# Head squares on GpSimd, an earlier centring, a later scaling and a shorter last norm in a two-block transformer kernel

## The chip, the cores and the metric

The kernel runs on one core of a Trainium2 chip. A core has five engines that work side by side, each with its own queue of instructions: TensorE (PE in the profile, PEld for its weight loads), VectorE (DVE), ScalarE (ACT), GpSimd (POOL) and SyncE (SP), which here issues the DMA transfers. They wait for each other by semaphores. The metric is the time of one launch in microseconds (us), as the median of several runs.

## The reference, cut to what matters

Everything is float32. A batch of B = 8 elements, each 512 tokens by 256 features, goes through two transformer blocks. The change touches block 0 alone, whose core is this (16 heads of 16 features each):

```python
h = modulate(ln(x), shift_sa, scale_sa)
q = ln(_heads(h, H)) * qn_w + qn_b          # a norm per token and head
k = ln(_heads(h, H)) * kn_w + kn_b
v = _heads(h, H)
attn = softmax(einsum('bhqd,bhkd->bhqk', q, k) * scale)
x = x + gate_sa[:, None, :] * unheads(einsum('bhqk,bhkd->bhqd', attn, v))
# cross-attention: q from modulate(ln(x), shift_ca, scale_ca), k and v from 64 context tokens
x = x + gate_ca[:, None, :] * (cross_attention(x) @ ca_out_w.T + ca_out_b)
h = modulate(ln(x), shift_ff, scale_ff)
x = x + gate_ff[:, None, :] * (silu(h @ w1.T) * (h @ w3.T) @ w2.T)
```

Each `ln` takes away the mean and divides by the standard deviation. `ln(_heads(h))` does so for each of the 16 features of a head, for 512 x 16 pairs of token and head. Block 1 has the same three stages with wider heads, and follows.

## The kernel before, in words

**Slots.** Block 0 is laid out by hand over slots. A cycle has 18 slots (`CYCLE`), one cycle for each batch element and two more to finish. In cycle b, `batch1(b)` does the self-attention of element b. Its 16 attention blocks (four groups g of four heads' work each, four pieces kt of the keys) fill the slots 0 to 8, 10 to 12 and 14 to 17. Slots 9 and 13 (`X0`, `X1`) hold the two cross-attention blocks of element b-1, which `batch2(b-1)` arranges. `batch3(b-2)` does the feed-forward part of element b-2 in the same cycle (for elements 5 and 6 three slots later, for element 7 two slots earlier). So three elements are in work at a time: in cycles 2 to 6 there are self-attention, cross-attention, feed-forward and the preparation of the next element. Cycles 0 and 1 have no feed-forward; from cycle 8 on there is no self-attention.

**Order.** `at(i, fn)` puts a piece of work beside slot i. A slot first issues the scores of its own block (TensorE) with their exponentials (ScalarE), then the values of the block before it, and then the pieces beside it in the order in which they were registered: all of `batch1`, then `batch2`, then `batch3`. The order of the instructions on TensorE, VectorE, ScalarE and GpSimd is exactly this written order; only the order of the DMA issues on SP is left to a planner. An instruction whose input is not ready holds up whatever is written behind it for the same engine.

**The head norm.** For elements from 1 on it is prepared in the cycle before. In slots counted from that cycle's start: `norm(0)`, `norm(1)`, `norm(2)` in 7, 8 and 9 (statistics of x, the layer norm into `ln`, then modulation on GpSimd into `h`, L504 and L506); `head_rows` in 12 (GpSimd zeroes the padding columns of the tile `zx`, L521); `head_centre` for both halves of the heads in 12 (VectorE: sums L528, means L529, and L530, which writes h minus mean into `zx`); `head_var` in 13 (ScalarE squares `zx` into `ln`, L536; VectorE sums, L538, and scales, L539); `head_scale` in 14 (GpSimd: a power, L545, and a product into `zx`, L546). Two slots before each group starts, `queries_keys(g)` transposes a part of `zx` on TensorE (L554) and makes q (ScalarE, L557) and k (VectorE, L558). For group 0 of the next element that is slot 16 of the cycle before; for groups 1, 2 and 3 it is slots 2, 6 and 12 of its own cycle. The tiles `zx` and `ln` have a single buffer each.

**PSUM.** `bank_x()` deals out PSUM banks in turn: two of the tag X and then one of the tag D. The transposes, projections and feed-forward steps all take theirs from it.

**Feed-forward.** `up(f)`, beside slot 8+f, multiplies by two weights on TensorE into two banks, takes tanh on ScalarE (L773), and then VectorE forms the products (L774 and L775), which read the banks and so free them. `down(t)` in slots 16 to 19 multiplies back, and `add_gated` (L460, L462) adds to x.

**Cross-attention.** `batch2(b)`, whose slots count from cycle b+1: `prepare(0..2)` in slots 3, 4, 5 (norm of x into z: statistics L199 and L201, the power L175, the normalisation L208; then on GpSimd the gate row, L675, and its addition to x, L437), `turn` in 6 (transposes of z, L416, and modulation, L417), `queries(0)` and `queries(1)` in 7 and 8, the blocks at `X0` and `X1`, `inverse(c)` three slots after its block (reciprocal L721 of the softmax sums, and two DMAs that spread them, L724 and L726), and `scaled(c)` five slots after it (VectorE, L729). The projection out (L741) comes in slots 1 and 2 of the next cycle.

```python
at(i - 6, head_rows)
for c in range(2):
    at(i - 6, lambda c=c: head_centre(c))
    at(i - 5, lambda c=c: head_var(c))
    at(i - 4, lambda c=c: head_scale(c))
```

Here i is the first slot of the element's own cycle, so i-6 is slot 12 of the cycle before.

Of the kernel before, what the change touches and what calls it, by code (L numbers as in the profile page):

```python
# [12 lines left out]
AF = mybir.ActivationFunctionType  # L13
ALU = mybir.AluOpType
# [3 lines left out]
B, N, D, H, T, CD, FF = 8, 512, 256, 16, 64, 192, 1024  # L18
# [60 lines left out]
def fast_path(ctx: ExitStack, tc: tile.TileContext, a: dict, out: bass.AP):  # L79

    nc = tc.nc
# [393 lines left out]
    def at(i, fn):  # L475
        beside.setdefault(max(i, -1), []).append(fn)
# [5 lines left out]
    def batch1(b):  # L482
        s = {}
        base = CYCLE * b
# [38 lines left out]
        def head_centre(c, par=None):  # L523

            hv = s["hv"][:, :, 8 * c : 8 * c + 8] if par is None else s["hv"][:, :, 8 * c + par : 8 * c + 8 : 2]
            sh = [P, NT, hv.shape[2]]
            mean = small.tile(sh, F32, tag=f"mean{sh[2]}", name="mean", bufs=2)
            nc.vector.tensor_reduce(mean, hv, AX.X, ALU.add)  # L528
            nc.vector.tensor_scalar_mul(mean, mean, 1.0 / HD0)  # L529
            nc.vector.tensor_tensor(parts(s["z"][:, :, 0:D], c, par), hv,  # L530
                                    mean[:, :, :, None].to_broadcast([*sh, HD0]), ALU.subtract)

        def head_var(c, par=None):
            sq, z = parts(s["ln"], c, par), parts(s["z"][:, :, 0:D], c, par)
            sh = [P, NT, z.shape[2]]
            nc.scalar.activation(sq, z, AF.Square)  # L536
            s["var", c, par] = var = small.tile(sh, F32, tag=f"var{sh[2]}", name="var", bufs=2)
            nc.vector.tensor_reduce(var, sq, AX.X, ALU.add)  # L538
            nc.vector.tensor_scalar(var, var, 1.0 / HD0, EPS0, ALU.mult, ALU.add)  # L539
# [71 lines left out]
        n = 0  # L611
        for g in range(4):
            for kt in range(NT):
                while n in (X0, X1):
                    n += 1
                i = base + n
                blocks[i] = block(g, kt)
                if g == 0 and kt == 0:
                    if b == 0:
                        def before():  # L620
                            head_rows()
                            for n in range(3):
                                norm(n)
                            nc.vector.tensor_copy(qk_cols, cols[:, 0:2])
                            first_modulated(0, 0)
                            head_centre(0, 0)
                            head_var(0, 0)
                            head_scale(0, 0, nc.vector)

                        def gate():  # L630
                            spread(s["bc"][:, 2 * D : 3 * D], b, G_SA, D)

                        at(-1, before)
                        at(0, lambda: awake(3))
                        at(0, lambda: first_modulated(0, 1))
                        at(0, lambda: head_centre(0, 1))
                        at(1, lambda: head_var(0, 1))
                        at(1, lambda: head_scale(0, 1))
                        at(2, lambda: first_modulated(1))
                        at(3, lambda: head_centre(1))  # L640
                        at(4, lambda: head_var(1))
                        at(4, lambda: head_scale(1))
                        at(5, gate)
                    else:
                        for m in range(3):
                            at(i - 11 + m, lambda m=m: norm(m))
                        at(i - 6, head_rows)
                        for c in range(2):
                            at(i - 6, lambda c=c: head_centre(c))
                            at(i - 5, lambda c=c: head_var(c))  # L650
                            at(i - 4, lambda c=c: head_scale(c))
                if kt == 0:
                    at(i - 2, lambda g=g: queries_keys(g))
                if kt == NT - 1:
                    at(i + 1, lambda g=g: group_end(g))
                    at(i + 2, lambda g=g: group_back(g))
                n += 1


    def batch2(b):  # L660
        s = {}
        base = CYCLE * (b + 1)

        def prepare(n):

            if n == 0:
                s["gate"] = gate = wk2.tile([P, D], F32, tag="gate", name="gate", bufs=3)
                spread(gate, b, G_CA, D)
                s["pieces"] = normed_in_pieces(wk2, b, EPS0, lambda z: s.update(z=z))
            s["pieces"][n]()  # L670
            if n < 2:
                return
            gate = s["gate"]
            gb = wk2.tile([P, D], F32, tag="gb", name="gb", bufs=1)
            nc.gpsimd.tensor_tensor(gb, gate, row("cab0"), ALU.mult)  # L675
            add_row(b, gb)

        def turn():
            s["hT"] = transposed(wk2, s["z"], b, modT[:, 2:4, :], modT[:, 0:2, :])

        def queries(c):
            ps = bank_x()
            for k in range(2):
                mm(ps, w_q0[:, k, c * P : (c + 1) * P], s["hT"][:, k, :], k == 0, k == 1)
            s[c] = q = wk2.tile([P, N], F32, tag="q0", name="q0", bufs=2)
            nc.vector.tensor_scalar_add(q, ps, col("bq")[:, c : c + 1])

        def block(c):
            def score():
                pss = [bank_s() for _ in range(2)]  # L690
                for j in range(4):
                    r = slice(32 * j, 32 * j + 32)
                    mm(pss[j // 2][:, j % 2, :], kb0[r, c, b, :, :].rearrange("p e t -> p (e t)"), s[c][r, :])
                for u in range(2):
                    s["p", c, u] = p = wk.tile([P, 2, N], F32, tag="p", name="p", bufs=4)
                    nc.scalar.activation(p, pss[u], AF.Exp, scale=HD0 ** -0.5)

            def value():
                o = bank_x()
                for j in range(4):  # L700
                    mm(o[32 * j : 32 * j + 32, :], vb0[:, b, 4 * c + j, :, :].rearrange("p e d -> p (e d)"),
                       s["p", c, j // 2][:, j % 2, :])
                s["oT", c] = oT = wk2.tile([P, N], F32, tag="oT0", name="oT0")
                nc.scalar.copy(oT, o)

                d = bank_x()
                for j in range(4):
                    mm(d[32 * j : 32 * j + 32, :], sel0, s["p", c, j // 2][:, j % 2, :])
                den = wk2.tile([P, N], F32, tag="den", name="den", bufs=1)
                nc.scalar.copy(den, d)  # L710
                s["den", c] = dd = dram.tile([4, 2, N], F32, tag="den0", name="den0")
                for e in range(2):
                    nc.sync.dma_start(dd[:, e, :], den.rearrange("(j r) n -> j r n", j=4)[:, e, :])
                s["rec", c] = rec = wk2.tile([P, 8 * N // P], F32, tag="rec", name="rec", bufs=2)
                nc.sync.dma_start(rec, flat(dd))

            return Block([score], [value])

        def inverse(c):
            rec = s["rec", c]  # L720
            nc.vector.reciprocal(rec, rec)  # L721
            s["rb", c] = rb = wk2.tile([P, N], F32, tag="rb", name="rb", bufs=1)
            rd = dram.tile([4, 2, N], F32, tag="rec0", name="rec0")
            nc.sync.dma_start(flat(rd), rec)  # L724
            check(rec)
            nc.sync.dma_start(rb, rd.rearrange("j e n -> (j e) n")[:, None, :].to_broadcast([8, HD0, N]))  # L726

        def scaled(c):
            nc.vector.tensor_tensor(s["oT", c], s["oT", c], s["rb", c], ALU.mult)  # L729

        for n in range(3):
            at(base + 3 + n, lambda n=n: prepare(n))
        at(base + 6, turn)
        at(base + 7, lambda: queries(0))
        at(base + 8, lambda: queries(1))
        for c, n in enumerate((X0, X1)):
            blocks[base + n] = block(c)
            at(base + n + 3, lambda c=c: inverse(c))
            at(base + n + 5, lambda c=c: scaled(c))
        for qp in range(2):  # L740
            at(base + CYCLE + 1 + qp, lambda qp=qp: project_out(qp, lambda k: s["oT", k], w_o0, 2,  # L741
                                                            add_gated(wk2, b, s["gate"])))
# [1497 lines left out]
```

## Time and profile before

| what | value |
|---|---|
| three runs | 2454.86, 2447.49, 2453.35 us; median 2453.35 |
| the profiled execution | 2448.82 us |
| its span, first to last instruction | 2446.9 us, mean granted TensorE clock 0.997 |
| busy: TensorE, VectorE, ScalarE, GpSimd | 2408.0, 1058.9, 878.5, 858.5 us |
| block 0 (TensorE goes on to block 1 without a stop) | to about 864 us |
| TensorE idle, 180 to 740 us | 1.6 us of 560 |
| the head norm's squares, L536 | 17 on ScalarE |

The profile is one execution of the kernel, with the start and the length of every instruction. Its page gives the busy time by engine, the chain of work that ended last, and groups of equal instructions. Further views list what an engine waited for and who released it ("PE ps_S L109 <- DVE k L558" is a matmul of line 109 into `ps_S` that waited for VectorE's write of `k` by line 558), the busy times by stretches of the span together with the clock granted to TensorE (1.00 is full), and the instructions in order of time. Such a line gives start, length, engine, source line, operation, output and inputs, shape, the count of instructions merged into the line, and in brackets the idle time of the engine before it with its releaser. Line 109 is the helper through which all matmuls go; which work it is, the names of its tiles tell.

### The profile page before, as it was taken

What the parts mean: (1) busy time and instruction counts of PE and PEld (TensorE: products, weight loads), DVE (VectorE), ACT (ScalarE), POOL (GpSimd) and SP (SyncE); (2) the same over time, 40 slices, a digit from 0 to 9 for tenths busy, and PEclk for the clock granted to TensorE, in tenths of its full rate; (3) what the DMA queues carried; (4) which work ended last, traced back from release to release, by engine and by line L of the source; (5) the groups of instructions that cost most, each with busy time, mean ns of one, the idle gap of its engine ahead of it and who ended that gap; (6) DMA issues with size and microseconds to landing.
All of it is one profiled execution on the core that took longest, in us unless ns stands there. A gap on an engine that the chain in (4) does not pass through costs nothing.

```text
span 2446.9 us, 28449 instructions
## 1 busy us (share of the span) xinstructions
PE 2408.0 (98%) x10964; PEld 1157.3 (47%) x10964; DVE 1058.9 (43%) x2083; ACT 878.5 (36%) x1118; POOL 858.5 (35%) x538
## 2 busy tenths in 40 slices
PE   9999999999998999999999999999999999999999
PEld 4333443444435643444444444434345555566665
DVE  5544435434434434343434343434334766651210
ACT  4565545545452123333333333333332221222221
POOL 3443222222301026343434343434333444531110
PEclk9999999999999999999999999999999999999999
DMA  5120000000001000000000000000123222210000
GB/s 181 45 93 7 16 20 8 17 11 12 13 11 64 27 1 23 18 19 19 19 18 19 18 19 19 19 18 19 36 61 96 68 67 67 64 55 27 22 18 23
DMA packets 84400, 84.07 MB, mean 34 GB/s; under 512 B 42544, under 2 KB 58784, under 8 KB 84256
## 3 DMA queue, kind: packets, MB, share of 16 engines
q1 hardware_dynamic: 83352, 81.09, 10.6%
q8 instruction: 88, 1.44, 0.2%
q10 hardware_dynamic: 904, 1.07, 0.1%
q14 instruction: 56, 0.46, 0.1%
HBM read 72.09 MB, written 10.04 MB: 34 GB/s over the span
## 4 chain that ended last, share of the span: by engine, by line
PE 92%; DVE 3%; issue 1%; ACT 1%; DMA 1%; POOL 1%; SPq 0%; POOLq 0%; DVEq 0%; ACTq 0%
PE ps_X L109 38%; PE ps_S L109 23%; PE ps_O L109 14%; PE ps_D L109 14%; PE ps_X L416 1%; DVE t L836 1%; DMA rec<-rec 1%; DMA rb<-rec 1%; POOL p L1252 1%; ACT p L574 0%; PE ps_X L554 0%; PE ps_X L596 0%; PE ps_D L416 0%; DVE t L833 0%; ACT hT L417 0%
## 5 line engine op out<-in xcount | busy, mean ns | idle before, releaser
L109 PE MATMUL ps_S<-q,k 32*128 32x512 f32 (+1 forms) x3072 | 429.1, 625 | 7.3 <-ACT p L574 3.1
L1012 ACT ACTIVATE p<-ps_S 128x1024 f32<-128x1024 f32 x256 | 248.1, 1022 | 522.1 <-PE ps_S L109 522.1
L574 ACT ACTIVATE p<-ps_S 128x1024 f32<-128x1024 f32 x256 | 248.2, 1021 | 232.1 <-PE ps_S L109 230.7
L109 PEld LDWEIGHTS ps_S<-q,k 32*128 32x128 f32 (+1 forms) x3072 | 160.5, 184 | 233.1 <-issue 137.5
L991 DVE TENSOR_TENSOR t<-ps_X,rope_c 128x512 f32<-128x512 f32 x126 | 87.2, 692 | 349.9 <-PE ps_X L109 349.9
L1031 DVE TENSOR_TENSOR sm<-sm,p 128x1024 f32<-128x1024 f32 x128 | 190.6, 1532 | 59.2 <-ACT p L1012 59.2
L994 POOL TENSOR_TENSOR q<-t 128x512 f32<-128x512 f32 x32 | 40.8, 1276 | 406.6 <-DVE t L992 406.6
L175 POOL TENSOR_TENSOR rstd<-rstd,mhalf 128x4 f32<-128x4 f32 x49 | 51.0, 1042 | 326.8 <-DVE rstd L174 325.2
L1027 POOL TENSOR_TENSOR sm<-p 128x1024 f32<-128x1024 f32 x64 | 149.3, 2354 | 38.0 <-ACT p L1012 38.0
L109 PE MATMUL ps_X<-hT,w 128*128 128x512 f32 x344 | 160.5, 601 | 1.3 <-ACT hT L417 0.9
L837 POOL TENSOR_TENSOR q<-t,t 128x512 f32<-128x512 f32 x72 | 95.1, 1321 | 176.4 <-DVE t L836 172.4
L109 PE MATMUL ps_O<-p,h 128*32 128x512 f32 x1024 | 139.4, 614 | 1.6 <-ACT oT L587 1.6
L109 PE MATMUL ps_O<-p,v 128*64 128x512 f32 x512 | 138.0, 617 | 0.0
L109 PE MATMUL ps_D<-p,v 128*64 128x512 f32 x512 | 131.6, 592 | 0.0
L453 DVE TENSOR_TENSOR x<-ps_X,x 128x512 f32<-128x512 f32 x27 | 18.7, 692 | 239.4 <-PE ps_X L109 239.4
L109 PE MATMUL ps_X<-hT,w_sa_wq 128*128 128x512 f32 x256 | 115.9, 595 | 3.0 <-ACT hT L417 3.0
L109 PE MATMUL ps_X<-w_sa_wv,hT 128*128 128x512 f32 x256 | 118.0, 604 | 0.0
L109 PE MATMUL ps_X<-w_sa_wo,oT 128*128 128x256 f32 x512 | 114.5, 382 | 0.1
L545 POOL TENSOR_TENSOR var<-var,mhalf 128x32 f32<-128x32 f32 (+1 forms) x17 | 87.3, 5135 | 75.2 <-ACT t L773 41.7
L109 PE MATMUL ps_X<-hT,w_sa_wk 128*128 128x512 f32 x248 | 112.4, 596 | 0.0
L109 PE MATMUL ps_S<-hT,w_ff_w 128*128 128x512 f32 x256 | 111.3, 592 | 0.0
L109 PEld LDWEIGHTS ps_X<-w_sa_wo,oT 128*128 128x128 f32 x512 | 96.0, 190 | 24.2 <-issue 11.4
(282 smaller groups left out, 3537.0 us busy)
## 6 DMA issues: line engine op xcount, KB each, us to landing
rb<-rec SPq DMA_DIRECT2D x128, 128.0 KB
rb<-rec_d SPq DMA_DIRECT2D x124, 128.0 KB
rb<-rec SPq DMA_DIRECT2D x16, 256.0 KB
out_dram<-x SPq DMA_DIRECT2D x15, 256.0 KB
x<-in_x_dram SPq DMA_DIRECT2D x7, 512.0 KB
bc<-modd SPq DMA_DIRECT2D x7, 384.0 KB
gate<-modd SPq DMA_DIRECT2D x16, 128.0 KB
k_d<-q SPq DMA_DIRECT2D x8, 256.0 KB
```

Of the source, the lines that this page charges most:

```text
L109: nc.tensor.matmul(o, lhsT, rhs, start=start, stop=stop)
L175: nc.gpsimd.tensor_tensor(r[:, :n], r[:, :n], mhalf[:, :n], ALU.pow)
L416: nc.tensor.transpose(ps[:, t * P : (t + 1) * P], z[:, t, k * P : (k + 1) * P], ident)
L545: nc.gpsimd.tensor_tensor(var, var, half, ALU.pow)
L574: nc.scalar.activation(pr[u], pss[u], AF.Exp, scale=HD0 ** -0.5)
L836: nc.vector.tensor_tensor(t2[d], ps[src], sn[src].to_broadcast([64, *shape[1:]]), ALU.mult)
L837: nc.gpsimd.tensor_tensor(dst, t1, t2, ALU.add)
L991: nc.vector.tensor_tensor(c, ps, rope_c, ALU.mult)
L994: nc.gpsimd.tensor_tensor(r[0], ec, os, ALU.subtract)
L1012: nc.scalar.activation(pr, pss[u], AF.Exp, scale=HD1 ** -0.5)
L1027: nc.gpsimd.tensor_tensor(sm, s["p", g, 0, u], s["p", g, 1, u], ALU.add)
L1031: nc.vector.tensor_tensor(s["sm", g, u], s["sm", g, u], s["p", g, t, u], ALU.add)
```

## The change

It has three parts, all in block 0.

1. The squares in `head_var` are formed as a product z times z on GpSimd for elements from 1 on (14 instructions of 128 x 512). For element 0 three stay on ScalarE. `norm(0..2)`, `head_rows` and `head_centre` of these elements come one slot earlier: slots 6, 7, 8 and 11 of the cycle before. `head_var` stays in slot 13 and `head_scale` in slot 14.
2. `scaled(0)` of the cross-attention comes seven slots after its block and no longer five: in slot 16, behind the `queries_keys(0)` of the next element, which `batch1` puts there. `scaled(1)` stays.
3. For the last element, the three pieces of `prepare` in `batch2` all come in slot 3, and `turn` and both `queries` one slot earlier each (5, 6, 7).

```diff
         def head_var(c, par=None):
             sq, z = parts(s["ln"], c, par), parts(s["z"][:, :, 0:D], c, par)
             sh = [P, NT, z.shape[2]]
-            nc.scalar.activation(sq, z, AF.Square)
+            if b:
+                nc.gpsimd.tensor_tensor(sq, z, z, ALU.mult)
+            else:
+                nc.scalar.activation(sq, z, AF.Square)
...
                         for m in range(3):
-                            at(i - 11 + m, lambda m=m: norm(m))
-                        at(i - 6, head_rows)
+                            at(i - 12 + m, lambda m=m: norm(m))
+                        at(i - 7, head_rows)
                         for c in range(2):
-                            at(i - 6, lambda c=c: head_centre(c))
+                            at(i - 7, lambda c=c: head_centre(c))
                             at(i - 5, lambda c=c: head_var(c))
                             at(i - 4, lambda c=c: head_scale(c))
...
+        early = b == B - 1
         for n in range(3):
-            at(base + 3 + n, lambda n=n: prepare(n))
-        at(base + 6, turn)
-        at(base + 7, lambda: queries(0))
-        at(base + 8, lambda: queries(1))
+            at(base + (3 if early else 3 + n), lambda n=n: prepare(n))
+        at(base + 6 - early, turn)
+        at(base + 7 - early, lambda: queries(0))
+        at(base + 8 - early, lambda: queries(1))
         for c, n in enumerate((X0, X1)):
             blocks[base + n] = block(c)
             at(base + n + 3, lambda c=c: inverse(c))
-            at(base + n + 5, lambda c=c: scaled(c))
+            at(base + n + (7, 5)[c], lambda c=c: scaled(c))
```

## The prediction

> **What bounds the kernel now.** I read the busy table first, then the chain that ended last:
>
> ```profile
> PE 2408.0 (98%) x10964; PEld 1157.3 (47%) x10964; DVE 1058.9 (43%) x2083; ACT 878.5 (36%) x1118; POOL 858.5 (35%) x538
> ...
> PE 92%; DVE 3%; issue 1%; ACT 1%; DMA 1%; POOL 1%; SPq 0%; POOLq 0%; DVEq 0%; ACTq 0%
> ```
>
> TensorE sets the end; the others are under half busy. Work moved between them is worth only the TensorE idle time that it removes or makes. The busy table by stretches shows where block 0 (to 864 us) has any (PE's sum is the second number, PEclk stands behind POOL):
>
> ```profile
> 60.00:120.00 60.00, 56.86 (x333) 20.12 (x332) 35.41 (x95) 35.16 (x41) 30.37 (x16) 0.97 0.14 42
> 120.00:180.00 60.00, 57.11 (x316) 19.25 (x315) 28.45 (x71) 35.78 (x43) 29.87 (x15) 0.91 0.29 99
> 180.00:740.00 560.00, 558.40 (x2875) 241.38 (x2872) 244.57 (x608) 287.20 (x357) 150.69 (x75) 1.00 0.04 12
> 740.00:790.00 50.00, 43.85 (x169) 23.48 (x168) 21.09 (x48) 12.13 (x17) 6.92 (x5) 0.97 0.11 35
> ```
>
> From 180 to 740 us, cycles 2 to 6, TensorE idles 1.6 us in 560: nothing to win, any wait is new loss. The list of waits names what idle time there is elsewhere (total, times, longest):
>
> ```profile
> PE ps_D L416 <- DVE z L208: 4.5, 1, 4.5
> PE ps_S L109 <- ACT p L574: 3.1, 7, 2.1
> PE ps_S L109 <- DVE k L558: 3.0, 3, 2.1
> ```
>
> The 4.5 lies at 752.53 to 757.06, where element 7's norm is late; the 2.1s at 72.5 (exponentials queued behind two squares on ScalarE) and at 157.2 (k queued behind the scaling of L729, which waited 8.19 us for a DMA).
>
> Last, the timeline of slot 12 of cycle 3, VectorE and TensorE around the centring:
>
> ```profile
> 413.24 0.66 PE L554 MATMUL ps_X<-ident,zx 128*128 128x128 f32 x4
> ...
> 413.73 1.88 PE L109 MATMUL ps_X<-hT,w 128*128 128x512 f32 x4
> 413.95 0.15 POOL L521 MEMSET zx<- 128x64 f32 x1 [11.11 <-PE ps_X L554]
> ...
> 416.70 0.69 DVE L530 TENSOR_TENSOR zx<-h,mean 128x512 f32<-128x512 f32 x1
> ...
> 417.31 0.68 DVE L528 TENSOR_REDUCE mean<-h 128x32 f32<-128x512 f32 x1
> 418.02 0.18 DVE L529 TENSOR_SCALAR mean<-mean 128x32 f32<-128x32 f32 x1
> 418.23 0.69 DVE L530 TENSOR_TENSOR zx<-h,mean 128x512 f32<-128x512 f32 x1
> 418.84 0.68 DVE L774 SCALAR_TENSOR_TENSOR t<-t,ps_X 128x512 f32<-128x512 f32 x1
> ```
>
> zx has one buffer. The last readers of element 3's zx are the transposes of its fourth group (L554) at 413.24 to 413.90. The zeroing for element 4 waited 11.11 us for them; L530 came after and never waited.
>
> [...] The trace agrees on 0.50 and on the step (half-clock stretches of 3.3, 10 and 3.3 us at 74.9, 156.8 and 757.4), but shows them after idle times of only 2.05, 2.09 and 4.53 us; idles up to 1.57 had none. [...] In the trace one L462 beside GpSimd's L609 took 1.12 us, not 0.69.
>
> **The change, part by part.** *Squares.* Fourteen leave ScalarE (0.64 us each, 9 us) for GpSimd. The trace has no square there; nearest is L546, a 128x512 product at 1.06 us (others of this size: 1.28, 1.32). I take 1.06, bounds 1.0 to 1.4. ScalarE's 9 us are worth nothing from 180 us on, TensorE being full. GpSimd's chain grows: in cycle 3 it ends at 435.55, the transposes that need it start at 438.05, so 2.5 us of cover. The squares (some 414.7 to 417.3) fall before the sums (L538) can start, behind the gate products of f4 at about 421, so the chain ends 0.3 to 2.2 us later. Cost nothing; without cover at most 2.
>
> *Centring one slot earlier.* L521 and both L528 to L530 go from slot 12 to slot 11. There they stand ahead of the transposes of the previous element's fourth group, which stay in slot 12 and read the one zx. So L530 now waits for a TensorE instruction that it preceded by nothing before. Ahead of it VectorE has finished by about 406; it stands until 413.9. Behind it are the second centring and the two products of feed-forward step f3 (L774, L775), which run at 410.19 and 411.27 now. They free the two PSUM banks (order X, X, D) that f4 takes on TensorE directly after those transposes. The price, by starts in the timeline: L530 at 413.95; to the next L528 0.61 (417.31−416.70), to L529 0.71, to L530 0.21, to L774 0.61, sum 2.14: L774 of f3 at 416.09, finished 416.77, f4 starts about 416.85 instead of 413.73. That is **3.1 us of idle TensorE**, in each cycle with feed-forward beside a next element: cycles 2 to 6, five times, **15.6 us**. [...] After it TensorE is behind, and nothing in 560 us of full work gives that back.
>
> *The clock.* 3.1 us of idleness exceeds the 2.05 that was enough three times of three. One window of 3.3 us at half clock loses 1.65: **8.3 us** for five. Bounds: nothing, and 5 each (as after 157.2), 25.
>
> *Cycle 0.* No feed-forward; behind the centring stands k of group 3. Its score goes from 67.89 to about 71.1, +3.2; the 2.05 wait behind the squares goes with its 1.65 of half clock (−3.7), but the new idle time may start a half window of its own (+1.65) and later work loses some slack: **+0.6**, bounds −0.5 and +2.5.
>
> *Cycle 1.* Here too k stands behind the centring: its score loses about 2.5 us, and perhaps a half window (1.65) or three (5). Against it, *scaling two slots later* puts L729 of group 0 behind k of the next element: the 2.09 at 157.2 and its half-clock stretch (5) should go, but the second half's recip and DMA chain (L729 at 163.11) keeps its time, so part of what is won waits there. 2.5 + 1.65 to 5 − 2.09 − 5 is −2.9 to +0.4: **−0.5**, bounds −5 and +9[...].
> In cycles 2 to 6 the scaling has slack of a cycle until L741's projection: nothing.
>
> *Last norm in one slot.* The second statistics at 753.90 stand behind L460, which waited 4.61 us for the down projection at 752.5. In slot 3 they stand before it: inputs done 747.07, statistics to about 749, power 1.02, four normalisations 1.78, z by 752, when TensorE reaches L416 (752.53). The 4.53 goes, and the half window at 757.4: **−6.2**. Bounds −6.5 and −3 (a later wait for the softmax DMA).
>
> Sum: 15.6 + 8.3 + 0.6 − 0.5 − 6.2 = **+17.8**. The profiled execution took 2448.8 (span 2446.9): it would take 2466.6. It lies 4.5 below the median, within the runs' scatter (2447.5 to 2454.9); on the median 2453.35 + 17.8 = **2471**.
>
> **Rivals.** (a) *Stalls without half clock*: 15.6 + 0.1 − 6.2, 2463, or 2458 with cycle 1's whole gain. [...] against it: three of three above 2 us. (b) *Longer half clock*, two or three windows after each stall[...]: 15.6 + 5×4 − 5, 2484. For it the 10 us at 156.8; against it the 3.3 at 757.4 and 74.9[...]. (c) *Faster*: f4 doesn't need the banks that f3's products free, or they come before L530 waits; then only cycle 1's −3 to −5 and the −6.2 stand, 2443. For it: two X banks, and no bank wait in this stretch now; against it: two X and one D are all there is, and f4 takes one of each kind right after f3 did. It decides once the five stalls together cost less than about 2, 0.4 each. (d) *GpSimd becomes the bound* at slot 16: if its chain grew by more than the 2.5 us and the 3.1 that TensorE slips; at a square of 3 us. Then 5×2 more, 2481. Speaks against it: half the span idle.
>
> **Numbers.** Main case 0.60; (a) 0.15; (b) 0.13; (c) 0.06; (d) 0.06. 0.3% is 7.4 us, about what a measurement of this kernel tells from no change. (c) ends faster mostly: 0.05. Half of (a), some of the rest and (c)'s remainder end within: 0.12. Slower 0.83. Range: down to (a)'s low end, 2457, up past (b) to 2488; outside it (c) and the tails.
>
> **What would show it.** TensorE waits of some 3.1 us before f4 for L779 (L774's line after), five, near 219, 316, 414 and so on, each later by what was lost before, and after each a granted clock of 0.50 for about 3.3 us; L530 with some 7 us of idle VectorE ahead of it, released by TensorE's zx transposes; 180 to 740 us stretched by 20 or so; no 4.5 us wait near 770, no k wait near 160. The prediction is wrong if f4 starts right after the transposes, if the clock stays full, or if the gain at the end is taken by the softmax DMA that follows it.

## The result and the profile after

| kernel | median (runs) | ratio to before, 95% interval |
|---|---|---|
| before | 2453.04 us (2447.49 to 2454.86, 4 runs) | |
| changed | 2478.19 us (2477.12 to 2479.23, 4 runs) | 1.0106 [1.0089, 1.0124] |

The change makes the kernel 25.2 us slower. The profiled execution of it took 2479.23 us, span 2477.4, against 2448.82 and 2446.9 before: 30.4 us more. It is the longest of the four runs of its kernel, and that of before was among the shorter of its own, so the traces show some 5 us more than the medians do.

The page's busy table for the changed kernel:

```profile
PE 2420.5 (98%) x10964; PEld 1161.9 (47%) x10964; DVE 1060.8 (43%) x2083; ACT 871.3 (35%) x1104; POOL 872.9 (35%) x552
```

The squares went from ScalarE to GpSimd, 7 and 14 us of busy time. TensorE is busy 12.5 us longer with the same 10964 matmuls: some ran at half clock (those at 436.15 below take 3.56 us instead of 1.88). The remaining 18 of the 30.5 us of span are new idle time. Both are seen in the stretches of block 0 (the second number is TensorE's busy time, the third last its granted clock):

```profile
60.00:120.00 60.00, 55.43 (x313) 20.01 (x312) 33.84 (x93) 32.91 (x37) 29.76 (x17) 0.91 0.14 40
120.00:180.00 60.00, 54.06 (x284) 18.60 (x283) 29.16 (x59) 30.93 (x36) 30.81 (x16) 0.89 0.28 98
180.00:740.00 560.00, 541.70 (x2769) 231.95 (x2769) 234.18 (x596) 274.62 (x335) 160.36 (x84) 0.98 0.04 12
740.00:790.00 50.00, 49.44 (x222) 27.07 (x221) 21.62 (x48) 13.83 (x19) 8.29 (x5) 1.00 0.04 12
```

TensorE idles 18.3 us between 180 and 740, where it idled 1.6. Its waits in block 0 (total, times, longest):

```profile
PE ps_X L109 <- DVE t L779: 10.0, 3, 3.3
PE ps_S L109 <- DVE k L561: 7.0, 3, 3.9
PE ps_D L109 <- DVE t L779: 6.7, 2, 3.3
PE ps_X L109 <- DVE oT L732: 2.9, 1, 2.9
...
PE ps_X L416 <- DVE z L208: 0.2, 1, 0.2
```

The three waits of the first line and the two of the third are the five stalls: in each, feed-forward step f4 waits 3.3 us for the first product of f3 (L779 is L774 of before, and L557 below is L554). The wait of L416 for z of 4.5 us is gone, and in its place stands 0.2. The timeline of slot 12 of cycle 3 in the changed kernel:

```profile
432.16 0.66 PE L557 MATMUL ps_X<-ident,zx 128*128 128x128 f32 x4
432.86 0.69 DVE L530 TENSOR_TENSOR zx<-h,mean 128x512 f32<-128x512 f32 x1 [6.80 <-PE ps_X L557]
...
433.46 0.68 DVE L528 TENSOR_REDUCE mean<-h 128x32 f32<-128x512 f32 x1
433.69 1.04 POOL L537 TENSOR_TENSOR ln<-zx 128x512 f32<-128x512 f32 x1 [0.66 <-DVE zx L530]
434.18 0.59 DVE L529 TENSOR_SCALAR mean<-mean 128x32 f32<-128x32 f32 x1
434.80 0.69 DVE L530 TENSOR_TENSOR zx<-h,mean 128x512 f32<-128x512 f32 x1
435.41 0.68 DVE L779 SCALAR_TENSOR_TENSOR t<-t,ps_X 128x512 f32<-128x512 f32 x1
...
436.15 3.56 PE L109 MATMUL ps_X<-hT,w 128*128 128x512 f32 x4 [3.33 <-DVE t L779]
```

VectorE stands 6.80 us until the transposes of the element before have read zx. Then the last step of the first centring (L530), the whole second centring and the product of f3 run one after the other, while TensorE waits. The four matmuls that follow take 3.56 us instead of 1.88: the record of the granted clock has 0.50 there for 3.4 us, from 435.9 on.

All 10964 matmuls come in the same order in both traces, so each can be compared with itself. The table says how much later they start, by stages (each number is what the stage adds, in us, in the two profiled executions):

| stage, by the time before | adds |
|---|---|
| cycle 0 (to 137) | +3.2 |
| cycle 1 (137 to 215) | +5.1 |
| cycles 2 to 6, the slots 12 (at 218, 316, 414, 511, 609) | +5.3, +5.3, +5.2, +6.7, +5.3, together 27.7 |
| last norm (740 to 802) | −6.3 |
| everything after | +0.3 |

### The profile page after: what moved, and what is told of

Same layout as the page of the kernel before. It is cut to its first block, busy times and chain, and to the rows that moved or that the text cites. A ratio compares the mean times of both kernels' runs of the same rounds, so it can differ in the third digit from the quotient of the medians.

```text
span 2477.4 us, 28450 instructions
## 1 busy us (share of the span) xinstructions
PE 2420.5 (98%) x10964; PEld 1161.9 (47%) x10964; DVE 1060.8 (43%) x2083; ACT 871.3 (35%) x1104; POOL 872.9 (35%) x552
## 4 chain that ended last, share of the span: by engine, by line
PE 91%; DVE 3%; DMA 2%; issue 1%; ACT 1%; POOL 1%; SPq 1%; POOLq 0%; DVEq 0%; ACTq 0%
PE ps_X L109 38%; PE ps_S L109 23%; PE ps_D L109 14%; PE ps_O L109 14%; PE ps_X L416 1%; DMA rb<-rec 1%; DVE t L841 1%; POOL p L1257 1%; DMA rec<-rec 1%; SPq L1250 1%; PE ps_X L557 0%; DVE zx L530 0%; ACT hT L417 0%; PE ps_X L599 0%; ACT p L577 0%
## 5 line engine op out<-in xcount | busy, mean ns | idle before, releaser
L109 PE MATMUL ps_X<-hT,w 128*128 128x512 f32 x344 | 168.2, 625 | 11.3 <-DVE t L779 10.0
L842 POOL TENSOR_TENSOR q<-t,t 128x512 f32<-128x512 f32 x72 | 94.5, 1312 | 180.5 <-DVE t L841 171.0
L109 PEld LDWEIGHTS ps_X<-hT,w 128*128 128x128 f32 x344 | 65.4, 198 | 102.4 <-issue 76.8
```

Source lines behind the costliest of these rows:

```text
L109: nc.tensor.matmul(o, lhsT, rhs, start=start, stop=stop)
L842: nc.gpsimd.tensor_tensor(dst, t1, t2, ALU.add)
```

## The experiments

All are the changed kernel with something undone, unless it is said that they start from the kernel before. Each ratio compares with runs of the kernel before that were taken beside it; their medians were 2450.0 to 2450.9 us.

**The centring alone put back**, with the zeroing of the padding. The early norms, the squares on GpSimd, the later scaling and the short last norm stay.

```diff
-                        at(i - 7, head_rows)
+                        at(i - 6, head_rows)
                         for c in range(2):
-                            at(i - 7, lambda c=c: head_centre(c))
+                            at(i - 6, lambda c=c: head_centre(c))
```

> The changed kernel with the zeroing and both centrings back in slot 12, behind the transposes; norms, squares on GpSimd, later scaling and short last norm stay. Theory (the place of the centring makes the loss): the five stalls and their half-clock windows (27.7 us by the two traces) go, and so do the added waits for k in cycles 0 and 1 (3.3 and up to 4.7); what stays is the gain at the end (5.7) and the squares no longer ahead of exponentials in cycle 0 (2.05 + 1.65). About 2440 to 2444 us. Rival (the squares on GpSimd, [...] make the loss): little comes back, above 2465.

Measured: 2442.46 us (7 runs), ratio to before 0.9972 [0.9961, 0.9984]. Its busy times by stretches show TensorE as full between 180 and 740 us as before, at full clock:

```profile
180.00:740.00 560.00, 558.39 (x2866) 243.32 (x2865) 241.28 (x598) 278.67 (x343) 162.49 (x84) 1.00 0.04 12
```

So the early place of the zeroing and centring makes the whole loss and more: without it the change is a gain of 7.5 us. This version is faster than both kernels.

**A second buffer for zx**, every instruction where the change put it; two other tiles give up a buffer to make room.

```diff
-            s["z"] = wk.tile([P, NT, DX], F32, tag="zx", name="zx", bufs=1)
+            s["z"] = wk.tile([P, NT, DX], F32, tag="zx", name="zx", bufs=2)
...
-                den = wk2.tile([P, N], F32, tag="den", name="den", bufs=1)
+                den = wk2.tile([P, N], F32, tag="tmp", name="den", bufs=1)
...
-                s["gate"] = gate = wk3.tile([P, D], F32, tag="gate3", name="gate3")
+                s["gate"] = gate = wk3.tile([P, D], F32, tag="gate3", name="gate3", bufs=1)
```

> The changed kernel with two buffers for zx, every instruction in the same order (to make room, den shares the buffer of tmp, and the feed-forward gate row has one buffer). Theory (L530 waits only because the transposes of the element before read the one zx): no idle of VectorE before L530, f4 starts at once, no half clock in cycles 2 to 6; cycles 0 and 1 lose nothing either. 2440 to 2446 us. Rival (the position in VectorE's order alone costs, wait or not): still above 2465.

Measured: 2444.04 us (7 runs), 0.9976 [0.9963, 0.9990]; TensorE is busy 558.40 of the 560 us. The earlier place costs nothing in cycles 2 to 6 once the buffer is free. It does not do better than putting the centring back, so the earlier start isn't worth anything either. In cycle 1 of its profile the projection waited 7.6 us for the second scaling, which comes at the end of a chain of DMAs; that chain is taken up again under cycle 1 below.

**The wait kept, the queue behind it emptied.** Both centrings stay in slot 11, but are registered last.

```diff
+    behind, after_rest = [], lambda i, fn: behind.append((i, fn))
...
-                            at(i - 7, lambda c=c: head_centre(c))
+                            after_rest(i - 7, lambda c=c: head_centre(c))
...
+    for i, fn in behind:
+        at(i, fn)
```

> The changed kernel with one thing moved: within slot 11 both centrings stand last, behind the products of f3 (in cycles 0 and 1 behind the context and key work of that slot). L530 still waits for the transposes, as long as before. Theory (not the wait itself but the queue behind it costs): f4 starts on time, no stall and no half clock in cycles 2 to 6, 27.7 us less; in cycles 0 and 1 k still stands behind the centrings, so 3.3 and up to 4.7 stay. About 2452 us (2448 to 2456). Rival (the wait itself holds up TensorE): no change, 2478.

Measured: 2442.44 us (6 runs), 0.9971 [0.9958, 0.9983]. The timeline of the same slot 12 in it:

```profile
408.45 0.69 DVE L779 SCALAR_TENSOR_TENSOR t<-t,ps_X 128x512 f32<-128x512 f32 x1 [3.92 <-ACT t L778]
...
411.50 0.66 PE L557 MATMUL ps_X<-ident,zx 128*128 128x128 f32 x4
412.00 1.88 PE L109 MATMUL ps_X<-hT,w 128*128 128x512 f32 x4
412.19 0.69 DVE L530 TENSOR_TENSOR zx<-h,mean 128x512 f32<-128x512 f32 x1 [1.15 <-PE ps_X L557]
```

L530 still starts only when the transposes have ended (VectorE now stands 1.15 us for them, not 6.80, since it has done f3's products first), and f4 starts at once. That L530 must wait for the transposes costs TensorE nothing; what stood behind it did. The time is 10 us below what was expected, since cycles 0 and 1 lost much less than in the changed kernel (+0.7 and −2.4 against before in the profiles, not +3.2 and +5.1), although k stands behind the centrings here too. More on that below.

**Half the queue.** Only the second centring goes behind f3's products (the list `behind` and the loop at the end are those of the run above).

```diff
-                            at(i - 7, lambda c=c: head_centre(c))
+                            (at if c == 0 else after_rest)(i - 7, lambda c=c: head_centre(c))
```

> The changed kernel with only the second centring moved behind the products of f3. The stall in cycles 2 to 6 should shorten from 3.3 us to that of one L530 and one L774-line product, 0.61 + 0.68 + some 0.1 and the start, 1.6 us. Theory (half clock comes with an idle time somewhere between 1.6 and 2.05 us or more): no half clock there, 5 x 1.6 = 8 us instead of 27.7, about 2459 us. Rival (any such idle time brings it): 8 + 8.5 us, about 2467.

Measured: 2456.28 us (9 runs), 1.0026 [1.0016, 1.0037]. Of the list of what TensorE waited for in this kernel:

```profile
PE ps_X L109 <- DVE t L779: 4.2, 3, 1.4
PE ps_D L109 <- DVE t L779: 2.8, 2, 1.4
```

Five waits of 1.4 us, and by the matmuls' starts each slot 12 adds 1.65 us; the granted clock from 180 to 740 us is 1.00, where it was 0.98. Shortening the stall by 1.9 us saves 3.6 in four of them and 5.0 in the one that had twice the half clock: what goes beyond 1.9 is the clock (an estimate: in the changed kernel the stretches of 3.4 and 6.8 us at 0.50 lose 1.7 and 3.4).

**The squares back on ScalarE**, the early centring kept.

```diff
-            if b:
-                nc.gpsimd.tensor_tensor(sq, z, z, ALU.mult)
-            else:
-                nc.scalar.activation(sq, z, AF.Square)
+            nc.scalar.activation(sq, z, AF.Square)
```

> The changed kernel with the squares back on ScalarE; the early centring stays. Theory (the early centring makes the stall, and the square on GpSimd only lengthens it by holding the mean's scaling L529 from 0.18 to 0.59 us): each of the five stalls falls from 3.3 to 2.9 us, still followed by half clock; 2 us less in all, about 2476 us. Rival (GpSimd's squares make the stall): the stalls go, about 2450 us.

Measured: 2470.81 us (4 runs), 1.0082 [1.0066, 1.0098]. The stalls stay; the timeline of slot 12 of cycle 3 (L779 of the changed kernel is L776 here):

```profile
423.33 0.18 DVE L529 TENSOR_SCALAR mean<-mean 128x32 f32<-128x32 f32 x1
...
424.15 0.68 DVE L776 SCALAR_TENSOR_TENSOR t<-t,ps_X 128x512 f32<-128x512 f32 x1
...
424.89 3.67 PE L109 MATMUL ps_X<-hT,w 128*128 128x512 f32 x4 [2.92 <-DVE t L776]
```

L529 takes 0.18 us again and the stall 2.92, so the square beside it cost 0.4 us. The kernel came out 5 us faster than expected. In its profile four slots 12 add 4.8 to 4.9 us each and the first only 3.2, which leaves 0.3 beyond its stall: there no half clock followed. Cycle 1 adds −1.0 instead of +5.1.

**The parts alone, on the kernel before.** First the last norm in one slot (the third part of the diff), then the later scaling, then the squares on GpSimd with the centring and the norms where they were.

> The kernel before with the last element's norm in one slot alone. Theory: the 4.53 us wait for z near 752 and the half-clock window after it go, 6 us less than before, and nothing else moves. Rival (a later wait for the softmax DMA takes it back): no difference.

Measured: 2444.67 us (15 runs), 0.9975 [0.9967, 0.9983], where before took 2450.87 beside it: 6.2 us less, and by the matmuls' starts the stage from 740 to 802 adds −6.25.

> The kernel before with the first scaling of cross-attention two slots later alone. Theory: in cycle 1 the wait of 2.09 us for k at 157 and its half-clock stretch go, but the second half's DMA chain then holds the projection; 1 to 5 us less than before. Rival (the DMA chain takes all of it): no difference.

Measured: 2449.46 us (21 runs), 0.9991 [0.9984, 0.9998]: 1.4 us less. The wait for k went, but one for the second scaling came. Of the list of waits:

```profile
PE ps_X L109 <- DVE oT L729: 2.1, 1, 2.1
```

> The kernel before with the squares on GpSimd alone, the centring where it was. Theory: only cycle 0 gains, 2.05 us of waiting behind two squares and the half window after it, some 3 us less than before; GpSimd's longer chain stays hidden in all later cycles. Rival (the longer GpSimd chain delays zx for the next group): slower than before, by 1 us in each of five cycles or more.

Measured: 2451.23 us (13 runs), 0.9998 [0.9989, 1.0006]: no difference, not the 3 us less. In its profile the wait behind the squares is gone, but cycle 0 gains only 1.0 and cycle 1 loses 1.8: its mean granted clock is 0.994, where the profile of before has 0.997. The longer GpSimd chain costs nothing in the five full cycles.

Together the three parts make −6.2, −1.4 and +0.4, which is −7.2 us. The kernel with the centring alone put back has all three, and the earlier norms besides, and is 7.5 us faster than before: the parts add up, and the earlier norms cost nothing that can be seen.

**The cycles apart**: the early centring for elements 1 and 2 only, and in a second run, with b > 2 in its place, for the others only.

```diff
-                        at(i - 7, head_rows)
+                        j = i - (7 if b < 3 else 6)
+                        at(j, head_rows)
                         for c in range(2):
-                            at(i - 7, lambda c=c: head_centre(c))
+                            at(j, lambda c=c: head_centre(c))
```

> The changed kernel with the early centring only for elements 1 and 2, that is in cycles 0 and 1; from element 3 on it is back in slot 12. Theory (the traces' own offsets: cycle 0 costs 5.6 and cycle 1 costs 7.7 us against the kernel with all centrings back, which took 2442.5): about 2455 us, with no stall in cycles 2 to 6. Rival (the forecast's terms for these cycles, +0.6 and -0.5): about 2450 us or less.

Measured: 2447.78 us (20 runs), 0.9987 [0.9980, 0.9994]: the early centring of cycles 0 and 1 costs 5.3 us against the kernel with all centrings back, not the 13.3 of the expectation. The profiles that this came from exaggerate: the one of the kernel with all centrings back is its fastest run (2439.42 us), with a granted clock of 1.00 in each of six stretches from 0 to 870 us.

> The changed kernel with the early centring only from element 3 on, that is in cycles 2 to 6. Theory: the five stalls of 3.3 us with a half-clock window each (5.2 to 6.7 by the trace) stand alone, 27.7 us on top of the 2442.5 with all centrings back: about 2470 us. Rival (later stalls are there only because the early cycles had fallen behind): below 2455 us.

Measured: 2470.97 us (4 runs), 1.0085 [1.0063, 1.0107]: 28.5 us on top of 2442.46. The stalls stand on their own. With the 5.3 it makes 2476.3, against the 2478.2 of the changed kernel: within the scatter of the runs the two groups of cycles add up.

## Why the prediction was right

The sign, the place and the mechanism were right, and the time lies in the range. 17.8 us were forecast, 25.2 measured. Of the 7.4 us that were missing, about half is in the two terms for the full cycles (27.7 us instead of 23.9) and half in those for cycles 0 and 1 (about 3.7 instead of 0.1); no two errors cancelled. The steps in turn:

**Five stalls, 15.6 us.** Right in kind, shown by three runs: they go when the centring goes back, when zx has two buffers, and when f3's products stand ahead. The 3.1 us each were 3.33: L529, the small scaling of the means, took 0.59 us beside the square where 0.18 was counted, and with the squares on ScalarE the stall is 2.92.

**The clock, 8.3 us.** Right in kind. One stretch of 3.3 us at half clock was forecast after each stall; in the changed kernel four were of 3.4 us and one was twice as long (6.8 us at 538). By the matmuls' starts stall and clock together are 27.7 us, by the run with the last five elements 28.5, against the 23.9 of the forecast's two terms.

**Cycle 0, +0.6, and cycle 1, −0.5.** These are the terms that were furthest off. Together they were put at +0.1 (the bound of +9 for cycle 1 was an estimate); the kernel with the early centring in these cycles alone is 2.5 us faster than before, of which the last norm is −6.2, so they cost about +3.7 (8.3 in the profile of the changed kernel, where cycle 0 with +3.2 lies above its bound of +2.5). In cycle 0 the score of group 3 starts at 70.98, as worked out (71.1), but the half-clock stretch beside it lasted 10.2 us, where one of 3.3 was taken:

```profile
70.98 2.09 PE L109 MATMUL ps_S<-q,k 16*128 16x512 f32 x8 [3.87 <-DVE k L561]
```

In cycle 1 the wait of 2.09 us and the half-clock stretch at 157 went as forecast, but came back as a wait for the second scaling. The step that failed is "keeps its time", said of that scaling: it came 6.6 us later. The forecast counted what k waits for, and left out what else stands behind the centring on VectorE in cycle 1: the products of the last cross-attention keys of block 1 (L833 and L836, in the changed kernel L838 and L841). Their sum on GpSimd (L842) is stored by SyncE (L864), and the loads of the feed-forward weights come behind that store in SyncE's queue. Of the timeline of SyncE and VectorE before:

```profile
137.87 2.66 SPq L859 DMA_DIRECT2D k_d<-q  x2
142.93 0.40 SPq L253 DMA_DIRECT2D w<-in_w1T_dram  x1
143.39 0.57 SPq L253 DMA_DIRECT2D w<-in_w3T_dram  x1
...
163.11 0.69 DVE L729 TENSOR_TENSOR oT<-oT,rb 128x512 f32<-128x512 f32 x1 [4.73 <-DMA rb<-rec]
```

And of the timeline of SyncE, VectorE and TensorE after:

```profile
139.43 9.12 SPq L864 DMA_DIRECT2D k_d<-q  x2
...
150.39 0.39 SPq L253 DMA_DIRECT2D w<-in_w1T_dram  x1
...
154.08 0.44 SPq L253 DMA_DIRECT2D w<-in_w3T_dram  x1
...
169.66 0.69 DVE L732 TENSOR_TENSOR oT<-oT,rb 128x512 f32<-128x512 f32 x1 [6.84 <-DMA rb<-rec]
170.41 2.93 PE L109 MATMUL ps_X<-w_o,oT 128*128 128x256 f32 x6 [2.85 <-DVE oT L732]
```

The line of 9.12 us holds two stores: the second waits for L842, which ends at 148.21, and is issued at 148.24, where it was at 140.21 before. The first two weights are issued 7.5 and 10.7 us later than before. The planner that orders SyncE's queue also gave this kernel another order: the second and third weights now stand among the small transfers of the second half's softmax sums and no longer ahead of them. The scaling that waits for these transfers comes 6.6 us later; TensorE, itself some 3.5 us late by then, waits 2.85 us for it and runs 10.2 us at half clock. Where the centring stands behind those products, k still waits 2.58 us, but the first weights are issued at 144.05, the scaling runs at 164.12, and cycle 1 takes 2.4 us less than before.

That the loads delay the small transfers fits four traces: before, with the third weight issued at 144.99 us, the second half takes 7.0 us from the issue of the transfer of its sums (rec from den) to its scaling; where that weight comes at 148.83 (two buffers), 151.64 (centring registered last) and 158.06 (changed kernel), all with the early centring in cycle 1, it takes 9.5, 10.1 and 12.0. This was not tried by itself, and the squares on ScalarE alone also brought cycle 1 from +5.1 to −1.0 in its profile, so what each cause is worth there stays open.

**Last norm, −6.2.** Right, with the edit alone: −6.2.

**Squares: nothing in the full cycles.** Right for the GpSimd chain. What they do add is the 0.4 us on L529, which costs only inside the stall.

**Rivals.** The stalls are not without half clock, so (a) is out. Half clock was not two or three times as long each time, so (b) is out, though once in five it was twice as long. Step f4 does need what f3's products free, so (c) is out, and GpSimd bounds nothing, so (d) is out.

## What to carry to other kernels

When a piece of work is moved forward in a queue that is served in order, look not for what it needs alone, but for what still reads the buffer that it writes, and then list everything behind it on its engine: there the wait is paid (here 6.80 us of VectorE's standing became 3.33 of TensorE's). A tile with one buffer ties the move to its last reader, wherever that stands. And go through that list to its end, over the engines and into the DMA queue: here a wait passed from VectorE to GpSimd to SyncE and on to loads that the forecast had not counted.

## What the runs showed of the hardware

Which waits of TensorE were followed by half clock: in the full cycles 2 to 6 none of the five waits of 1.4 us (half the queue) was, four of the five of 2.92 us (squares on ScalarE, by what each slot 12 added) and all five of 3.33 us of the changed kernel were, four times for 3.4 us and once for 6.8. Why the first of the five of 2.92 us was not stays open.

In the traces before and after, all 11 half-clock stretches (without the last microseconds of each) last one, two or three times 3.413 us, and in each trace they begin whole multiples of that step apart, to within 0.002 us. On this grid each of the five waits of 3.33 us leaves 2.51 to 3.12 us of idle TensorE in one step at full clock, and the next step is at half clock. At 538 the end of the wait reached 0.64 us into the half-clock step, and a second one followed; in the other four it reached 0.21 us or less, and full clock came back. This is read from the traces afterwards; no run moved a wait along the grid.

Idle time in the step alone does not settle it: before, a step with only 1.2 us of idle TensorE (from 71.3) was followed by half clock, and one with 1.48 us (from 750.6) was not. In cycles 0 and 1 a stretch lasted up to 10.2 us, also through steps that the trace shows without idle time (from 160.1 before, from 74.1 after); what keeps it going stays open. The runs of one kernel lie up to 9 us apart, and their granted clocks differ: of the 42 runs of before taken beside the squares alone, the shortest has 2445.59 us and a mean clock of 0.998, the longest 2453.93 us and 0.994. Whether all of the scatter comes from it was not shown.

A GpSimd product of 128x512 with both inputs in SBUF took 1.04 us, and beside it a VectorE scaling of 128x32, from SBUF to SBUF, took 0.59 instead of 0.18 us. The reduction (L528) that ran as the product started kept its 0.68. The scaling ended as GpSimd's product did (434.77 and 434.73). It did so in all five full cycles, and in the run with the centring registered last it took 1.17 us beside a GpSimd sum of 1.26 us and again ended with it (141.47 and 141.42). In the run with the squares on ScalarE, with no GpSimd product beside it, it took 0.18 (at 423.33).
